# Three-layer CIN on one core: one gather row for both weights of a pair, W2 in one transfer, two field tiles ahead of the weight table

## The chip, the cores and the metric

The kernel runs on one core of a Trainium2 chip. The metric is the device time of one execution in microseconds (us), the median of nine runs. Engines are named as in the profile: PE is TensorE (PEld its weight loads), DVE is VectorE, ACT is ScalarE, POOL is GpSimd, SP is the sync engine. A name with q, as SPq, is an engine's instruction queue where it issues a DMA or waits.

## The reference

What is computed is a compressed interaction network of three layers on an embedding x of shape (1024, 39, 64), batch by fields by embedding:

```python
def _cin_layer(Xk, X0, W, b):
    O = W.shape[0]
    Hk, Fdim = (Xk.shape[1], X0.shape[1])
    Wr = W.reshape(O, Hk, Fdim)
    return jnp.einsum('bhe,bfe,ohf->boe', Xk, X0, Wr) + b[None, :, None]
X0 = sparse_embedding
Xk = X0
outs = []
for W, b in ((W0, b0), (W1, b1), (W2, b2)):
    Xk = _cin_layer(Xk, X0, W, b)
    outs.append(Xk.sum(axis=-1))
cin_output = jnp.concatenate(outs, axis=-1)
return cin_output @ fc_w.T + fc_b
```

W0 is (64, 39*39), W1 and W2 are (64, 64*39), fc_w is (1, 192), all in float32.

## The kernel before

**The mathematics.** The last two layers are linear in the layer before, and only their sum against fc_w is wanted. So the kernel folds W2 with fc_w into a matrix v2, and W1 with v2 into one weight per pair of fields. Each pair of fields (a, b) then has 128 weights: 64 of the first layer (from W0) and 64 of the folded rest. The main loop multiplies the products of field pairs with them. A pair (a, b) and a pair (b, a) have the same product, so their weights are added first.

**The main loop.** The batch is worked in 32 blocks of 32 samples, 2048 columns each. A block has six products of 128 pairs each (`PAIRS`, steps in the order 0, 1, 3, 2, 4, 5); a seventh product serves two blocks, 64 rows for each. `product` forms one on DVE from two tiles of gathered field rows: `rt[n % 2][:, i]`, i from 0 to 3, for the six, `ut` and `vt` for the seventh. `multiply` runs it through PE, four quarters of 512 columns, each of two passes. `finish` and `finish_quarter` multiply the two halves of the result and sum over the embedding. At the start the order is: three steps of block 0, three of block 1, then the rest of block 0, the seventh product, and the rest of block 1. Four product buffers exist (`prods`), and products are formed four steps ahead (`AHEAD`).

**How field rows arrive.** `load(n)` copies block n of x from HBM to a table `xd` in HBM, in pieces of 256 B, so that each field is a row of 8 KB. `roll(n, tiles)` then has POOL gather 128 such rows per tile by an indirect DMA (`lists` holds the row numbers), `roll_half(n)` does so for `ut` and `vt`.

**How weights arrive.** A second table in HBM, `table`, has a row of 128 floats for each ordered pair of fields (40 x 40 rows). It is written from the tiles `part` (two groups of 16 columns) and `rest` by three DMAs. `weights(c)` gathers from it twice for each of seven chunks, `wa` for (a, b) and `wb` for (b, a), by the row numbers in `wlists`; `add(c)` on DVE adds the two.

**The start.** All this is preceded by a chain of small steps, written out by hand on each queue. W2 is loaded in two halves of 64 partitions (`halves`), and so is W1. `fc2` holds a part of fc_w, copied there by ACT. Matmuls with `fc2` (line 278) fold W2; DVE transposes the result (line 289); `v2` takes it; matmuls with `v2` (lines 322 and 331) fold W1. `spin` runs matmuls without use, to keep PE at work. ACT copies W0 from `w0s` and `w0r` into `part` and `rest`, and DVE and ACT copy the folded part beside it. Then the table is written and gathered.

**What sets the order.** Each engine and each DMA-issuing queue works in program order (`manual_schedule`); waits between engines come from the tiles' accesses. DMAs of SP and ACT share eight semaphores in turn, and those of POOL another eight; a DMA waits until the earlier one of its semaphore has landed.

Of the kernel before, what the change touches and what calls it, by code (L numbers as in the profile page):

```python
# [58 lines left out]
FH = F * H  # L59
# [36 lines left out]
def cin_kernel(ctx: ExitStack, tc: tile.TileContext, x, w0t, b0, w1, b1, w2, b2, fc_w, fc_b, out):  # L96
# [16 lines left out]
    def load(n, engine=nc.sync):  # L113
        first = n % 2 * FT
        engine.dma_start(
            xd[n // 2 % NTAB][first : first + F].rearrange("f (b e) -> f b e", e=E),
            xv[:, n * BB : (n + 1) * BB, :],
        )
# [7 lines left out]
    def roll(n, tiles=range(4)):  # L126
        for i in tiles:
            gather_rows(rt[n % 2][:, i], n, n % 2 * 4 + i)
# [4 lines left out]

    wa = const.tile([128, NCHUNK, 2 * H], F32, name="wa")
    wb = const.tile([128, NCHUNK, 2 * H], F32, name="wb")
    fc = const.tile([H, 3], F32, name="fc")
# [7 lines left out]
    lists = const.tile([128, 10], I32, name="lists")  # L144
    wlists = const.tile([128, 2, NCHUNK], I32, name="wlists")
    rt = [const.tile([128, 4, BLK], F32, name=f"r{k}") for k in range(2)]
    ut = [const.tile([128, BLK], F32, name=f"u{k}") for k in range(2)]
    vt = [const.tile([128, BLK], F32, name=f"v{k}") for k in range(2)]

    table = dram.tile([FT * FT, 2 * H], F32, name="table")  # L150
    tablev = table.rearrange("(b a) h -> b a h", a=FT)

    prep = tc.tile_pool(name="prep", bufs=1)
    with prep as prep:
        w2s = prep.tile([128, FH // 2], F32, name="w2s")
        w1s = prep.tile([128, FH // 2], F32, name="w1s")
        fc2 = prep.tile([128, 32], F32, name="fc2")
        ones = prep.tile([16, 128], F32, name="ones")
# [7 lines left out]


        nc.gpsimd.iota(place, pattern=[[0, 1]], base=0, channel_multiplier=1)
        nc.vector.memset(warm, 0.0)
        nc.vector.memset(zeros, 0.0)  # L170
        nc.vector.memset(fc2, 0.0)  # L171
        nc.vector.memset(ones, 1.0)
        load(0, nc.gpsimd)
        nc.gpsimd.memset(w0s, 0.0)
        nc.gpsimd.memset(w0r, 0.0)
        load(1, nc.gpsimd)
        nc.gpsimd.memset(v2, 0.0)
        nc.gpsimd.memset(rest[:, NR], 0.0)

        def halves(dst, w):  # L180
            for s in range(2):
                nc.sync.dma_start(
                    dst[H * s : H * s + H], w[:, s * (FH // 2) : (s + 1) * (FH // 2)]
                )

        def load_ones(k, engine):
            for row in (F, FT + F):
                engine.dma_start(xd[k][row].rearrange("(p c) -> p c", c=128), ones)

        halves(w2s, w2)  # L190
        halves(w1s, w1)
        nc.scalar.dma_start(fc, fc_w.rearrange("o (l h) -> h (o l)", h=H))
        load_ones(0, nc.scalar)
        nc.scalar.copy(warm, warm)
        for k in range(2):
            nc.scalar.dma_start(w0s[H * k : H * k + F], w0t[:, NA * k : NA * (k + 1), :])
        nc.scalar.dma_start(w0r[0:F], w0t[:, 2 * NA : F, :])
        for s in range(2):
            nc.scalar.copy(fc2[H * s : H * s + H, 0:1], fc[:, 2:3])  # L199
            nc.scalar.copy(v2[H * s : H * s + H, F:FT], fc[:, 1:2])  # L200
# [8 lines left out]
        def spin(n):  # L209
            for _ in range(n):  # L210
                nc.tensor.matmul(idle, zeros[:, 0:128], zeros, start=True, stop=True)  # L211
# [14 lines left out]
        def step(x, at, by, out=None):  # L226

            out = new() if out is None else out
            nc.vector.tensor_scalar(out, x, at, by, ALU.is_ge, ALU.mult)
            return out  # L230

        def fused(out, x, scalar, y, op0, op1):
            nc.vector.scalar_tensor_tensor(out, x, scalar, y, op0, op1)
# [19 lines left out]
        nc.vector.tensor_scalar(lists[:, 4:8], fields_of[:, 0:4], float(FT), None, ALU.add)  # L253
        roll(0, (0, 1, 2))
        roll(1, (0, 1))

        step(row, HR, 1.0, half)
        fused(q, half, -float(HR), row, ALU.mult, ALU.add)
        nc.vector.tensor_tensor(field[4], q, step(q, F, -float(F)), ALU.add)
        nc.vector.tensor_tensor(field[4], field[4], step(q, 56, 11.0), ALU.add)  # L260
        nc.vector.tensor_scalar(field[5], q, float(F), None, ALU.min)
        fused(t, q, -50.0, step(q, 45, 1.0), ALU.add, ALU.mult)
        for y in (t, step(q, 50, -float(F)), step(q, 56, -6.0)):
            nc.vector.tensor_tensor(field[5], field[5], y, ALU.add)

        nc.vector.tensor_scalar(half, half, float(FT), None, ALU.mult)
        nc.vector.tensor_scalar(lists[:, 8:10], fields_of[:, 4:6], half, None, ALU.add)

# [5 lines left out]
        for k in range(2):  # L274
            for u in range(4):
                rows = slice(u % 2 * H, u % 2 * H + H)
                f0 = u // 2 * 19 + k * 10
                nc.tensor.matmul(  # L278
                    pv[k][32 * u : 32 * u + 32, 0:320],
                    fc2[rows],  # L280
                    w2v[rows, f0 : f0 + 10, :],
                    start=True,
                    stop=True,
                )
# [13 lines left out]

        nc.vector.tensor_scalar(scaled, fields_of, float(FT), None, ALU.mult)
        pair = prep.tile([128, 4], F32, name="pair")  # L300
        nc.vector.tensor_scalar(wlists[:, 0, 0:3], scaled[:, 1:4], field[0], None, ALU.add)
        nc.vector.tensor_scalar(wlists[:, 1, 0:3], fields_of[:, 1:4], scaled[:, 0:1], None, ALU.add)
        nc.vector.tensor_tensor(wlists[:, 0, 3:5], scaled[:, 2:4], fields_of[:, 1:3], ALU.add)
        nc.vector.tensor_tensor(wlists[:, 1, 3:5], scaled[:, 1:3], fields_of[:, 2:4], ALU.add)
        for m, (i, k) in enumerate(((1, 3), (3, 1), (4, 5), (5, 4))):
            nc.vector.tensor_tensor(pair[:, m : m + 1], scaled[:, k : k + 1], field[i], ALU.add)
        fused(wlists[:, 0, 5:6], extra, float(NONE), pair[:, 0:1], ALU.mult, ALU.max)
        fused(wlists[:, 1, 5:6], extra, float(NONE), pair[:, 1:2], ALU.mult, ALU.max)
        last = step(q, 62, float(NONE))
        nc.vector.tensor_tensor(wlists[:, 0, 6:7], pair[:, 2:3], last, ALU.max)  # L310
        nc.vector.tensor_scalar(t, q, float(F), float(NONE), ALU.is_lt, ALU.mult)
        nc.vector.tensor_tensor(pair[:, 3:4], pair[:, 3:4], t, ALU.max)
        nc.vector.tensor_tensor(wlists[:, 1, 6:7], pair[:, 3:4], last, ALU.max)

# [14 lines left out]
        for s in range(2):  # L329
# [3 lines left out]
            )  # L333
        spin(9)
        for s, copy in enumerate((nc.vector.tensor_copy, nc.scalar.copy)):
# [5 lines left out]
            )  # L341
        nc.sync.dma_start(tablev[:, 0:NA, :], part[0:FT])
        nc.scalar.dma_start(tablev[:, NA : 2 * NA, :], part[H : H + FT])
        nc.sync.dma_start(tablev[:, 2 * NA : FT, :], rest[0:FT])
        for k in range(1, NTAB):
# [3 lines left out]
    def weights(c):  # L349
        for k, w in enumerate((wa, wb)):  # L350
            nc.gpsimd.indirect_dma_start(  # L351
                w[:, c], None, table[:], bass.IndirectOffsetOnAxis(ap=wlists[:, k, c : c + 1], axis=0)
            )

    weights(0)
    weights(1)
    weights(3)
    roll(1, (2,))
    weights(2)
    roll(0, (3,))  # L360
    weights(4)
    weights(5)
    roll_half(0)
    weights(6)
    roll(1, (3,))
# [16 lines left out]
    def multiply(n, c, p, quarters=range(BLK // MM)):  # L382
        half = c == NPAIR
        for k in (n, n + 1) if half else (n,):
            if k not in po:
                po[k] = [bank("po") for _ in range(BLK // MM)]
        for m in quarters:

            for h in range(2 if half else 1):
                w = slice(h * HR, (h + 1) * HR) if half else slice(0, 128)  # L390
                nc.tensor.matmul(  # L391
                    po[n + h][m],
                    wa[w, c, :],
                    p[w, bass.ts(m, MM)],
                    start=c == opens[n + h],
                    stop=c == closes[n + h],
                )
# [47 lines left out]

    def add(c):
        nc.vector.tensor_tensor(wa[:, c], wa[:, c], wb[:, c], ALU.add)

    AHEAD = 4
# [14 lines left out]
    last_weights()  # L464
    p = {s: product(*s) for s in steps[:2]}
    added = set()

    def add(c):
        if c not in added:
            added.add(c)  # L470
            nc.vector.tensor_tensor(wa[:, c], wa[:, c], wb[:, c], ALU.add)  # L471

    add(steps[0][1])
    p[steps[2]] = product(*steps[2])
    add(steps[1][1])
    add(steps[2][1])
    p[steps[3]] = product(*steps[3])
    fields(0)
# [76 lines left out]
```

## Time and profile before

| | us |
|---|---|
| median of nine runs (lowest, highest) | 766.96 (765.55, 768.89) |
| the profiled execution, its own time | 765.15 |
| its span in the profile | 763.3 |
| PE busy | 745.1 |
| main loop's matmuls (line 391), busy | 724.1 |
| DVE busy | 641.4 |
| POOL busy | 321.4 |
| table's DMAs issued | 16.84 to 17.68 |
| first gather from the table issued | 28.09 |
| first main matmul | 33.98 |

Times in the profile are counted from the start of its span; the execution's own time is 1.85 us longer than the span. A group's line gives its busy time and the idle time of its engine just before it, with what ended that wait. A piece of the chain says when it began, how long it took and which instruction or transfer it was. PE's matmuls of 32-bit floats appear as two records each. The granted clock of PE is 1 or one half; the mean was 0.991.

### The profile page before, as it was taken

The numbers are of one execution on the slowest core, as the hardware profiler recorded it, in microseconds if no ns is written. First come the engines' busy times: TensorE is split into PE (matmuls) and PEld (weight loads), VectorE is DVE, ScalarE is ACT, GpSimd is POOL, SyncE is SP. The second block draws the span as 40 slices with busy tenths as digits, with TensorE's granted clock in tenths as the row PEclk, the third lists the DMA queues.
The fourth block names the chain that finished last, engine by engine and source line by source line (L and its number), as shares of the span: only waits on it lengthen the run. The fifth ranks groups of instructions, "written<-read, shape, count | busy, mean of one in ns | idle before, by whom it ended". The sixth has DMA issues, their size and how long they took to land.

```text
span 763.3 us, 5146 instructions
## 1 busy us (share of the span) xinstructions
PE 745.1 (98%) x1856; PEld 322.3 (42%) x1856; DVE 641.4 (84%) x479; ACT 160.4 (21%) x207; POOL 321.4 (42%) x185
## 2 busy tenths in 40 slices
PE   6599999999999999999999999999999999999998
PEld 2244444444444444444444444444444444444443
DVE  6376988898888888988888988888998888898885
ACT  2002312211221211222121222212122221212212
POOL 4488173633436354243625425363432536334200
PEclk9799999999999999999999999999999999999999
DMA  8849968565876657687575768657577764737400
GB/s 259 270 172 392 389 212 333 188 276 185 327 253 233 263 188 271 213 330 248 203 288 167 273 244 321 237 190 291 177 282 253 282 261 155 272 151 311 166 0 0
DMA packets 62839, 181.79 MB, mean 238 GB/s; under 512 B 41364, under 2 KB 41499, under 8 KB 42254
## 3 DMA queue, kind: packets, MB, share of 16 engines
q0 software_dynamic: 23712, 169.34, 57.9%
q1 hardware_dynamic: 38494, 11.36, 6.4%
q10 hardware_dynamic: 608, 0.77, 0.3%
q8 instruction: 14, 0.23, 0.1%
q14 instruction: 11, 0.09, 0.0%
HBM read 180.58 MB, written 11.10 MB: 251 GB/s over the span
## 4 chain that ended last, share of the span: by engine, by line
PE 92%; DMA 4%; issue 2%; POOL 1%; DVE 0%; ACT 0%; SPq 0%; POOLq 0%; DVEq 0%
PE po L391 91%; DMA table<-rest 1%; DMA u<-xd,lists 1%; POOL wb L351 1%; DMA fc<-in_fc_w 1%; POOL wa L351 1%; DMA b0s<-in_b 1%; DMA wa<-table,wlists 1%; DMA wb<-table,wlists 0%; PE pv L278 0%; PE pt L322 0%; POOL r L122 0%; DVE blocks L289 0%; PE pr L331 0%; DVE g L430 0%
## 5 line engine op out<-in xcount | busy, mean ns | idle before, releaser
L391 PE MATMUL po<-p,wa 128*128 128x512 f32 (+1 forms) x1792 | 724.1, 596 | 9.0 <-DVE wa L471 9.0
L377 DVE TENSOR_TENSOR p<-r 128x2048 f32<-128x2048 f32 x192 | 434.6, 2290 | 91.0 <-PE po L391 83.8
L391 PEld LDWEIGHTS po<-p,wa 128*128 128x128 f32 (+1 forms) x1792 | 314.9, 190 | 417.5 <-issue 395.8
L122 POOL DMA_INDIRECT r<-xd,lists x128 | 249.7, 1951 | 362.3 <-DVE p L377 335.9
L410 ACT ACTIVATE x<-po,b0s 64x512 f32<-64x512 f32 x124 | 84.5, 684 | 354.4 <-PE po L391 347.9
L404 ACT COPY g<-u 39x1024 f32<-39x1024 f32 x64 | 66.6, 1043 | 215.0 <-DVE sums L421 181.2
L416 DVE SCALAR_TENSOR_TENSOR g<-po,fc,x 64x512 f32<-64x512 f32 x124 | 86.4, 734 | 0.0
L421 DVE TENSOR_REDUCE sums<-g 103x16 f32<-103x1024 f32 x62 | 75.6, 1220 | 2.2
L379 DVE TENSOR_TENSOR p<-u,v 128x2048 f32<-128x2048 f32 x16 | 36.5, 2284 | 5.5 <-DMA v<-xd,lists 5.5
L122 POOL DMA_INDIRECT u<-xd,lists x16 | 30.7, 1919 | 4.9 <-issue 4.6
L122 POOL DMA_INDIRECT v<-xd,lists x16 | 16.0, 999 | 4.9 <-issue 4.9
L351 POOL DMA_INDIRECT wa<-table,wlists x7 | 10.5, 1503 | 14.2 <-DMA table<-rest 12.4
L211 PE MATMUL idle<-zeros 128*128 128x512 f32 x24 | 13.1, 692 | 1.5 <-DVE fc L171 1.5
L351 POOL DMA_INDIRECT wb<-table,wlists x7 | 10.3, 1478 | 2.1 <-issue 2.1
L471 DVE TENSOR_TENSOR wa<-wa,wb 128x128 f32<-128x128 f32 x7 | 2.0, 286 | 9.1 <-DMA wa<-table,wlists 7.0
L211 PEld LDWEIGHTS idle<-zeros 128*128 128x128 f32 x24 | 5.0, 220 | 8.2 <-issue 6.8
L430 DVE SCALAR_TENSOR_TENSOR g<-po,fc,x1q 64x512 f32<-64x512 f32 x4 | 3.0, 743 | 5.3 <-ACT x1q L429 5.3
L278 PE MATMUL pv<-w2s,fc 64*32 64x320 f32 x16 | 2.8, 764 | 4.4 <-DMA b0s<-in_b 4.4
L289 DVE STREAM_TRANSPOSE blocks<-pv 64x320 f32<-64x320 f32 x4 | 2.1, 514 | 3.7 <-issue 3.5
L429 ACT ACTIVATE x1q<-po,b0s 64x512 f32<-64x512 f32 x4 | 2.7, 684 | 10.2 <-PE po L391 10.2
L278 PEld LDWEIGHTS pv<-w2s,fc 64*32 64x32 f32 x16 | 1.0, 142 | 6.6 <-ACT fc L199 6.0
L432 DVE TENSOR_REDUCE sums<-g 103x8 f32<-103x512 f32 x4 | 2.7, 686 | 0.1
(74 smaller groups left out, 30.4 us busy)
## 6 DMA issues: line engine op xcount, KB each, us to landing
xd<-in_x SPq DMA_DIRECT2D x30, 312.0 KB
r<-xd,lists POOLq DMA_INDIRECT x128
w2s<-in_w SPq DMA_DIRECT2D x2, 312.0 KB
xd<-in_x POOLq DMA_DIRECT2D x2, 312.0 KB
w1s<-in_w SPq DMA_DIRECT2D x2, 312.0 KB
table<-part SPq DMA_DIRECT2D x1, 320.0 KB
table<-part ACTq DMA_DIRECT2D x1, 320.0 KB
w0s<-in_w0t ACTq DMA_DIRECT2D x2, 156.0 KB
```

Source lines behind the costliest of these rows:

```text
L122: nc.gpsimd.indirect_dma_start(dst, None, table, bass.IndirectOffsetOnAxis(ap=lists[:, k : k + 1], axis=0))
L211: nc.tensor.matmul(idle, zeros[:, 0:128], zeros, start=True, stop=True)
L278: nc.tensor.matmul(pv[k][32 * u : 32 * u + 32, 0:320], fc2[rows], w2v[rows, f0 : f0 + 10, :], start=True, stop=True,)
L351: nc.gpsimd.indirect_dma_start(w[:, c], None, table[:], bass.IndirectOffsetOnAxis(ap=wlists[:, k, c : c + 1], axis=0))
L377: nc.vector.tensor_tensor(p, rt[n % 2][:, i], rt[n % 2][:, k], ALU.mult)
L379: nc.vector.tensor_tensor(p, ut[n // 2 % 2], vt[n // 2 % 2], ALU.mult)
L391: nc.tensor.matmul(po[n + h][m], wa[w, c, :], p[w, bass.ts(m, MM)], start=c == opens[n + h], stop=c == closes[n + h],)
L404: nc.scalar.copy(gt[H : H + F], ut[n // 2 % 2][h : h + F, bass.ts(m, SUB)])
L410: nc.scalar.activation(x1[m // 2][:, bass.ts(m % 2, MM)], po[n][m][H:128], AF.Identity, bias=b0s[H:128])
L416: nc.vector.scalar_tensor_tensor(gt[0:H, at], po[n][m][0:H], fc[:, 0:1], x1[m // 2][:, at], ALU.add, ALU.mult)
L421: nc.vector.tensor_reduce(sums[:, b_at : b_at + SB], gt.rearrange("p (b e) -> p b e", e=E), AX.X, ALU.add)
L430: nc.vector.scalar_tensor_tensor(gt[0:H], po[n][m][0:H], fc[:, 0:1], t, ALU.add, ALU.mult)
```

## The change

The table's row is doubled to 256 floats: the first half of row (b, a) holds that pair's weights, the second half those of (a, b). Each half ("side") is written by its own three DMAs, six in all. One gather per chunk brings both halves into one tile `w`, and `add` adds the second half to the first; for the seventh chunk it adds under a mask, `apart`. The second list of row numbers goes away.

In the start, W2 comes in one transfer of 128 partitions in which output and half alternate; `fc2` is widened, spread to suit, and filled by two DMAs instead of ACT's copies; the line-278 matmuls take all 128 rows. load(0) moves from POOL to SP, behind W2. W1's halves and W0's parts are split over SP and ACT. Some memsets move from POOL to DVE. The list arithmetic for `lists[:, 8:10]` and `wlists` is done later. Ahead of the table POOL gathers two tiles (block 0, tiles 0 and 1) instead of five; block 0's tile 2 comes after weights(0), load(1) after weights(1), and block 1's tiles 0 to 2 after weights(3). weights(6) comes ahead of roll_half(0). `spin(9)` becomes `spin(13)`.

```diff
-    table = dram.tile([FT * FT, 2 * H], F32, name="table")
-    tablev = table.rearrange("(b a) h -> b a h", a=FT)
+    table = dram.tile([FT * FT, 4 * H], F32, name="table")
+    sides = (
+        table.rearrange("(b a) h -> b a h", a=FT)[:, :, 0 : 2 * H],
+        table.rearrange("(a b) h -> b a h", b=FT)[:, :, 2 * H : 4 * H],
+    )
...
-        load(0, nc.gpsimd)
         nc.gpsimd.memset(w0s, 0.0)
         nc.gpsimd.memset(w0r, 0.0)
-        load(1, nc.gpsimd)
-        nc.gpsimd.memset(v2, 0.0)
-        nc.gpsimd.memset(rest[:, NR], 0.0)
...
-        halves(w2s, w2)
-        halves(w1s, w1)
-        nc.scalar.dma_start(fc, fc_w.rearrange("o (l h) -> h (o l)", h=H))
+        fcv = fc_w.rearrange("o (l h) -> h (o l)", h=H)
+        for s, engine in enumerate((nc.sync, nc.scalar)):
+            engine.dma_start(fc2[s:128:2, 32 * s : 32 * s + 1], fcv[:, 2:3])
+        nc.sync.dma_start(w2s, w2.rearrange("o (s n) -> (o s) n", s=2))
+        nc.scalar.dma_start(fc, fcv)
+        load(0)
         load_ones(0, nc.scalar)
+        for s, engine in enumerate((nc.sync, nc.scalar)):
+            engine.dma_start(
+                w1s[H * s : H * s + H], w1[:, s * (FH // 2) : (s + 1) * (FH // 2)]
+            )
+        for k, engine in enumerate((nc.sync, nc.scalar)):
+            engine.dma_start(w0s[H * k : H * k + F], w0t[:, NA * k : NA * (k + 1), :])
+        nc.sync.dma_start(w0r[0:F], w0t[:, 2 * NA : F, :])
         nc.scalar.copy(warm, warm)
...
-            nc.scalar.copy(fc2[H * s : H * s + H, 0:1], fc[:, 2:3])
...
-        roll(0, (0, 1, 2))
-        roll(1, (0, 1))
...
+        roll(0, (0, 1))
...
-                    fc2[rows],
-                    w2v[rows, f0 : f0 + 10, :],
+                    fc2[:, u % 2 * 32 : u % 2 * 32 + 32],
+                    w2v[:, f0 : f0 + 10, :],
...
-        spin(9)
+        spin(13)
...
-        nc.sync.dma_start(tablev[:, 0:NA, :], part[0:FT])
-        nc.scalar.dma_start(tablev[:, NA : 2 * NA, :], part[H : H + FT])
-        nc.sync.dma_start(tablev[:, 2 * NA : FT, :], rest[0:FT])
+        for k, engine in enumerate((nc.sync, nc.scalar)):
+            for side in sides:
+                engine.dma_start(side[:, NA * k : NA * (k + 1), :], part[H * k : H * k + FT])
+        for side, engine in zip(sides, (nc.sync, nc.scalar)):
+            engine.dma_start(side[:, 2 * NA : FT, :], rest[0:FT])
...
     def weights(c):
-        for k, w in enumerate((wa, wb)):
-            nc.gpsimd.indirect_dma_start(
-                w[:, c], None, table[:], bass.IndirectOffsetOnAxis(ap=wlists[:, k, c : c + 1], axis=0)
-            )
+        nc.gpsimd.indirect_dma_start(
+            w[:, c], None, table[:], bass.IndirectOffsetOnAxis(ap=wlists[:, c : c + 1], axis=0)
+        )
 
     weights(0)
+    roll(0, (2,))
     weights(1)
+    load(1, nc.gpsimd)
     weights(3)
-    roll(1, (2,))
+    roll(1, (0, 1, 2))
     weights(2)
     roll(0, (3,))
     weights(4)
     weights(5)
+    weights(6)
     roll_half(0)
-    weights(6)
     roll(1, (3,))
     load(2)
     load(3)
...
-            nc.vector.tensor_tensor(wa[:, c], wa[:, c], wb[:, c], ALU.add)
+            one, other = w[:, c, 0 : 2 * H], w[:, c, 2 * H : 4 * H]
+            if c < NPAIR:
+                nc.vector.tensor_tensor(one, one, other, ALU.add)
+            else:
+                nc.vector.scalar_tensor_tensor(one, other, apart, one, ALU.mult, ALU.add)
```

More of the change, by code (lines that the diff above doesn't have):

```diff
@@ L132, in roll_half @@
         gather_rows(vt[n // 2 % 2], n, 9)
-    wa = const.tile([128, NCHUNK, 2 * H], F32, name="wa")
-    wb = const.tile([128, NCHUNK, 2 * H], F32, name="wb")
+    w = const.tile([128, NCHUNK, 4 * H], F32, name="w")
     fc = const.tile([H, 3], F32, name="fc")
@@ L144, in cin_kernel @@
     lists = const.tile([128, 10], I32, name="lists")
-    wlists = const.tile([128, 2, NCHUNK], I32, name="wlists")
+    wlists = const.tile([128, NCHUNK], I32, name="wlists")
+    apart = const.tile([128, 1], F32, name="apart")
     rt = [const.tile([128, 4, BLK], F32, name=f"r{k}") for k in range(2)]
@@ L156, in cin_kernel @@
         w1s = prep.tile([128, FH // 2], F32, name="w1s")
-        fc2 = prep.tile([128, 32], F32, name="fc2")
+        fc2 = prep.tile([128, H], F32, name="fc2")
         ones = prep.tile([16, 128], F32, name="ones")
@@ L168, in cin_kernel @@
         nc.gpsimd.iota(place, pattern=[[0, 1]], base=0, channel_multiplier=1)
[L169 to L172, printed above, removed]
-        load(0, nc.gpsimd)
         nc.gpsimd.memset(w0s, 0.0)
         nc.gpsimd.memset(w0r, 0.0)
-        load(1, nc.gpsimd)
-        nc.gpsimd.memset(v2, 0.0)
-        nc.gpsimd.memset(rest[:, NR], 0.0)
[L180 to L183, printed above, removed]
-                )
+        nc.vector.memset(fc2, 0.0)
+        nc.vector.memset(zeros, 0.0)
+        nc.vector.memset(warm, 0.0)
+        nc.vector.memset(ones, 1.0)
+        nc.vector.memset(v2, 0.0)
+        nc.vector.memset(rest[:, NR], 0.0)
         def load_ones(k, engine):
@@ L188, in load_ones @@
                 engine.dma_start(xd[k][row].rearrange("(p c) -> p c", c=128), ones)
-        halves(w2s, w2)
-        halves(w1s, w1)
-        nc.scalar.dma_start(fc, fc_w.rearrange("o (l h) -> h (o l)", h=H))
-        load_ones(0, nc.scalar)
+        fcv = fc_w.rearrange("o (l h) -> h (o l)", h=H)
[4 more added lines that the diff above has]
+        load(0)
+        load_ones(0, nc.scalar)
+        for s, engine in enumerate((nc.sync, nc.scalar)):
[5 more added lines that the diff above has]
+        nc.sync.dma_start(w0r[0:F], w0t[:, 2 * NA : F, :])
         nc.scalar.copy(warm, warm)
-        for k in range(2):
-            nc.scalar.dma_start(w0s[H * k : H * k + F], w0t[:, NA * k : NA * (k + 1), :])
-        nc.scalar.dma_start(w0r[0:F], w0t[:, 2 * NA : F, :])
         for s in range(2):
-            nc.scalar.copy(fc2[H * s : H * s + H, 0:1], fc[:, 2:3])
             nc.scalar.copy(v2[H * s : H * s + H, F:FT], fc[:, 1:2])
@@ L253, in cin_kernel @@
         nc.vector.tensor_scalar(lists[:, 4:8], fields_of[:, 0:4], float(FT), None, ALU.add)
-        roll(0, (0, 1, 2))
-        roll(1, (0, 1))
[L257 to L267, printed above, removed]
+        roll(0, (0, 1))
         blocks = prep.tile([H, F * 32], F32, name="blocks")
@@ L275, in cin_kernel @@
             for u in range(4):
-                rows = slice(u % 2 * H, u % 2 * H + H)
                 f0 = u // 2 * 19 + k * 10
@@ L296, in cin_kernel @@
         nc.scalar.copy(rest[:, 0:NR, H : 2 * H], w0r.rearrange("b (a h) -> b a h", h=H))
[L299 to L313, printed above, removed]
+        step(row, HR, 1.0, half)
+        fused(q, half, -float(HR), row, ALU.mult, ALU.add)
+        nc.vector.tensor_tensor(field[4], q, step(q, F, -float(F)), ALU.add)
+        nc.vector.tensor_tensor(field[4], field[4], step(q, 56, 11.0), ALU.add)
+        nc.vector.tensor_scalar(field[5], q, float(F), None, ALU.min)
+        fused(t, q, -50.0, step(q, 45, 1.0), ALU.add, ALU.mult)
+        for y in (t, step(q, 50, -float(F)), step(q, 56, -6.0)):
+            nc.vector.tensor_tensor(field[5], field[5], y, ALU.add)
+        nc.vector.tensor_scalar(half, half, float(FT), None, ALU.mult)
+        nc.vector.tensor_scalar(lists[:, 8:10], fields_of[:, 4:6], half, None, ALU.add)
         w1v = w1s.rearrange("o (h f) -> o f h", f=F)
@@ L341, in cin_kernel @@
             )
-        nc.sync.dma_start(tablev[:, 0:NA, :], part[0:FT])
-        nc.scalar.dma_start(tablev[:, NA : 2 * NA, :], part[H : H + FT])
-        nc.sync.dma_start(tablev[:, 2 * NA : FT, :], rest[0:FT])
+        for k, engine in enumerate((nc.sync, nc.scalar)):
[3 more added lines that the diff above has]
+            engine.dma_start(side[:, 2 * NA : FT, :], rest[0:FT])
+        nc.vector.tensor_scalar(scaled, fields_of, float(FT), None, ALU.mult)
+        pair = prep.tile([128, 2], F32, name="pair")
+        nc.vector.tensor_scalar(wlists[:, 0:3], scaled[:, 1:4], field[0], None, ALU.add)
+        nc.vector.tensor_tensor(wlists[:, 3:5], scaled[:, 2:4], fields_of[:, 1:3], ALU.add)
+        for m, (i, k) in enumerate(((1, 3), (4, 5))):
+            nc.vector.tensor_tensor(pair[:, m : m + 1], scaled[:, k : k + 1], field[i], ALU.add)
+        fused(wlists[:, 5:6], extra, float(NONE), pair[:, 0:1], ALU.mult, ALU.max)
+        fused(wlists[:, 6:7], step(q, 62, 1.0), float(NONE), pair[:, 1:2], ALU.mult, ALU.max)
+        step(q, F, 1.0, apart)
         for k in range(1, NTAB):
@@ L349, in weights @@
     def weights(c):
-        for k, w in enumerate((wa, wb)):
-            nc.gpsimd.indirect_dma_start(
-                w[:, c], None, table[:], bass.IndirectOffsetOnAxis(ap=wlists[:, k, c : c + 1], axis=0)
-            )
+        nc.gpsimd.indirect_dma_start(
+            w[:, c], None, table[:], bass.IndirectOffsetOnAxis(ap=wlists[:, c : c + 1], axis=0)
+        )
     weights(0)
+    roll(0, (2,))
     weights(1)
+    load(1, nc.gpsimd)
     weights(3)
-    roll(1, (2,))
+    roll(1, (0, 1, 2))
     weights(2)
@@ L389, in multiply @@
             for h in range(2 if half else 1):
-                w = slice(h * HR, (h + 1) * HR) if half else slice(0, 128)
+                rows = slice(h * HR, (h + 1) * HR) if half else slice(0, 128)
                 nc.tensor.matmul(
                     po[n + h][m],
-                    wa[w, c, :],
-                    p[w, bass.ts(m, MM)],
+                    w[rows, c, 0 : 2 * H],
+                    p[rows, bass.ts(m, MM)],
                     start=c == opens[n + h],
@@ L444, in last_weights @@
         nc.scalar.activation(kfin, pk[0:1, 0:1], AF.Identity, bias=fcb, scale=float(E))
-    def add(c):
-        nc.vector.tensor_tensor(wa[:, c], wa[:, c], wb[:, c], ALU.add)
     AHEAD = 4
@@ L464, in cin_kernel @@
     last_weights()
-    p = {s: product(*s) for s in steps[:2]}
+    p = {steps[0]: product(*steps[0])}
     added = set()
@@ L470, in add @@
             added.add(c)
-            nc.vector.tensor_tensor(wa[:, c], wa[:, c], wb[:, c], ALU.add)
+            one, other = w[:, c, 0 : 2 * H], w[:, c, 2 * H : 4 * H]
[3 more added lines that the diff above has]
+                nc.vector.scalar_tensor_tensor(one, other, apart, one, ALU.mult, ALU.add)
     add(steps[0][1])
[L474 to L477, printed above, removed]
+    for k in (1, 2, 3):
+        p[steps[k]] = product(*steps[k])
+        if k < 3:
+            add(steps[k][1])
     fields(0)
```

## The prediction

> **What bounds the kernel now.** I read the page's busy times first, then the chain of waits, then the timeline of the first 70 us, then what the DMA queues moved in single stretches.
>
> ```profile
> PE 745.1 (98%) x1856; PEld 322.3 (42%) x1856; DVE 641.4 (84%) x479; ACT 160.4 (21%) x207; POOL 321.4 (42%) x185
> L391 PE MATMUL po<-p,wa 128*128 128x512 f32 (+1 forms) x1792 | 724.1, 596 | 9.0 <-DVE wa L471 9.0
> ```
>
> TensorE works for 724.1 us in the main loop and waits 9.0 us ahead of it, 8.7 of them before its first matmul. From there to the end of the loop it has no other hole than 0.27 us. So the change, which touches only the start, moves the end by what it moves the moment from which TensorE never waits again. The timeline gives the stations on the way:
>
> ```profile
> 9.67 1.04 POOL L122 DMA_INDIRECT r<-xd,lists  x1 [4.46 <-DMA xd<-in_x]
> 9.68 2.83 PE L278 MATMUL pv<-w2s,fc 64*32 64x320 f32 x16 [4.41 <-DMA b0s<-in_b]
> ...
> 16.88 7.99 PE L211 MATMUL idle<-zeros 128*128 128x512 f32 x18
> ...
> 28.09 0.94 POOL L351 DMA_INDIRECT wa<-table,wlists  x1 [12.36 <-DMA table<-rest]
> ...
> 33.98 11.44 PE L391 MATMUL po<-p,wa 128*128 128x512 f32 x19 [8.78 <-DVE wa L471]
> ...
> 37.16 0.95 POOL L122 DMA_INDIRECT r<-xd,lists  x1 [0.30 <-DMA wa<-table,wlists]
> ...
> 47.60 2.29 DVE L377 TENSOR_TENSOR p<-r 128x2048 f32<-128x2048 f32 x1 [0.23 <-PE po L391]
> ...
> 64.65 0.28 DVE L471 TENSOR_TENSOR wa<-wa,wb 128x128 f32<-128x128 f32 x1
> 64.99 45.27 PE L391 MATMUL po<-p,wa 128*128 128x512 f32 x119 [0.27 <-DVE wa L471]
> ```
>
> Fields' weights start at 9.68, the table's last write is issued at 17.41, POOL gathers from it at 28.09, TensorE starts at 33.98. The product at 47.60 waits for a free buffer, which is the end of the third step (0,3): so step (1,0) starts at about 47.4. Adding the 0.27 hole, the old schedule counts as one in which (1,0) starts at **47.6** and nothing waits later. That is the number to beat.
>
> ```profile
> 17.41 9.96 DMA table<-rest
> 33.10 3.85 DMA wa<-table,wlists
> 52.27 6.88 DMA u<-xd,lists
> ```
>
> The longest piece of the chain is the table's landing. The five gathers ahead of it and the table share the DMA engines:
>
> ```profile
> DMA packets 367, 2.74 MB, mean 343 GB/s; under 512 B 32, under 2 KB 32, under 8 KB 32
> q0 software_dynamic: 366, 2.74, 100.5%
> ```
>
> This is 12 to 20 us: POOL's queue alone fills all 16 engines.
>
> [...] the landing records of the first write of part hold ten increments, 24.19 to 25.17 us. [...] packets of 8192 B take 309 ns, of 512 B 27 ns, of 256 B 18 ns. [...] w2s ran at 199 GB/s from 2 to 5 us, gathers into 128 partitions at 343[...]. [...] Here it was half from 29.9 to 40.1 us, after the spins ended at 24.9.
>
> **W2 and x.** Before, w2s landed by 6.88, but the matmuls at 9.68 waited for ACT's copies of fc, queued behind ACT's w0s issue at 8.06. Now fc2 is filled by two small DMAs (0.6 us of issue each, as a bias load), so w2s is issued at 1.6 instead of 0.74. With eight packets per engine from about 3.0 and the same 1 us from last packet to landing I put it at 6.2 (bounds 5.5 and 7.6), hence pv at 6.6: 3.1 us earlier. It also falls into full clock, -0.5 us on the way to pt (bounds 0 and -0.9). Matmuls of 128 rows instead of 64 are taken as equal in time, since the old row shows 16 of 763 ns in 2.83 us, four or so at once (bounds -0.9 and +1.4, half the row). load(0) goes from POOL to SP, behind w2s on one queue: data 6.0 to 7.8, landing 1 us later, so the first gather is issued at about 8.8 instead of 9.67 (bounds 7.8 and 10.3). w1s's second half, w0s, bias wait for an earlier DMA of the same semaphore, as bias did before (1.3 us behind fc); w1s should land near 10, just as v2 is ready at 6.6+3.7=10.3. ACT's copy of w0s into part (1.05) must come before its pt copy; w0s lands by 11, which leaves a microsecond. The list arithmetic that moved (14 small DVE instructions of 0.15, 2 us) lies under pt and pr (3 us); if that cover is gone it adds 2 us at most. memsets moved to DVE: 0.4 us, before the lists, which are ready at 6.1, still before load(0). The old last issue was 7.73 after pv began; now, with one more DMA on each queue (0.6), it is 6.6+7.73-0.5+0.6 = 14.4, the first at 13.2.
>
> **The table.** Bytes double to 1.64 MB, and rows of 1 KB with a half written by each side turn 8 KB packets into 512 B ones: 3200 on ten engines is 320 each, by 27 ns = **8.6 us** (before: 40+40 of 8192 B and 40 of 4096 B, 4 each: 4x309x2+4x159 = 3.1 us of work, but shared with gathers). Two gathers precede it instead of five. In the old trace two took from 11.44 to 18.0; 0.9 earlier they end at 17.1. The old table's first packet came 3.9 us after its issue, behind gathers; 13.2+3.9 = 17.1 too. So the table has the engines to itself from 17.1, ends 25.7, lands 0.9 later (as before): **T = 26.6** against 27.37. Bounds: gathers over at 15.5 and 25 ns each give 24.4; 29 ns and a start at 18 give 28.2; strided HBM writes have no row here, 36 ns would give 29.5.
>
> **After the table.** POOL spends 1.25 us per gather (0.95+0.30). Seven gathers fewer free 8.8 us of POOL time, but what matters is the order. From T: weights(0) at +0.7, r0 tile 2 to +2.9, weights(1), load(1) to +5.6. weights(0) is one gather: landing +4.3, add, first matmul at +4.9 (old +6.6). Its step needs r0 tile 2 next: landing +7.5 (the tile issued at 37.16 landed at 42.76, 4.65 after its issue ended), product +9.9; at half clock step (0,0) ends at +11.8 anyway. Three steps of 3.43 plus about 3 of cold clock end at +18.2. Block 1 is now late: roll(1) may only start when load(1) has landed. POOL's old loads landed 5.6 and 6.3 us after their issue ended: +11.2. Tiles 0 and 1 are issued to +12.5 and +13.7; the first lands 4.65 later, the second 3.25 after it (as v after u), +20.4; product 2.29: (1,0) starts at **T+22.7**. TensorE stands still for some 4.5 us there. What is queued behind POOL's wait, weights(2), r0 tile 3, u, v, is needed at +32.9 or later and lands by +26 to +33; u and v are needed at +43. [...]
>
> The sum: 26.6+22.7 = 49.3 against 47.6 is +1.7 us[...]. **+2.0 us**. On the profiled execution (765.15, span 763.3) that is 767.2; it was 1.8 under the median, so on 766.96 it is **769.0**.
>
> **Rivals.** Faster: the table is out early. If load(0) lands at 7.8 and the gathers end at 15.5, T is 24.4, and if load(1), with no W1 or W2 beside it, lands 4 us after issue, (1,0) starts at T+21.1 = 45.5: -2.1 us, 764.9. For it: the idle engines after T (36 to 39 us of the old trace moved a mean of 54 GB/s). Against it: 4992 packets of loads 2 to 5 come at that time. It decides where T plus the delay falls under 47.6 - 1.5 = 46.1. No difference: T=26, delay 21.6, +0.0, 767.0; early start and late block 1 cancel. Much slower: 512 B writes at 36 ns, T=29.5, (1,0) at 52.2: +4.6, 771.6. That the seven gathers themselves bring time is excluded by the waits: only weights(0) is on the path, where it saves 1.25.
>
> **Chances.** About 0.2% (1.5 us) is what a measurement of this kernel can tell from no change. Slower by more: 0.54 (the likeliest, 768.5 to 772; with small writes slow up to 774). Within: 0.26. Faster: 0.20. Range 764.8 to 773.0.
>
> **To check.** pv near 6.6; first gather near 8.8; last table landing near 26.6; no spin longer than to 25; first main matmul near 31.5; a hole of 4 to 5 us ahead of (1,0) with its product waiting for a landing of r, POOL waiting there for xd; no hole later. Wrong if the table lands before 25 or load(1) holds nobody up.

## The result and the profile after

The changed kernel takes **771.86 us** (median of ten executions, 771.05 to 774.45) against 766.97 for the kernel before (31 executions): ratio 1.0063, 95% interval 1.0050 to 1.0075, so 4.9 us slower. Its profiled execution took 772.29, with a span of 770.5.

The page's busy times and the main loop's group, as before:

```profile
PE 750.7 (97%) x1864; PEld 324.4 (42%) x1864; DVE 640.8 (83%) x474; ACT 159.9 (21%) x205; POOL 310.7 (40%) x175
L389 PE MATMUL po<-p,w 128*128 128x512 f32 (+1 forms) x1792 | 726.6, 598 | 12.3 <-DVE w L468 8.2
```

The main loop's idle time is 12.3 us instead of 9.0: 8.2 ahead of the first matmul, and a new 4.1. The timeline (start, duration, engine, what it does, in brackets the wait ahead of it and its releaser) shows the stations. A step (n, c) is product c of block n, and T is the landing of the last table write:

```profile
7.78 2.56 PE L266 MATMUL pv<-w2s,fc 128*32 128x320 f32 x16 [2.46 <-DMA w2s<-in_w]
...
10.83 1.10 POOL L122 DMA_INDIRECT r<-xd,lists  x1 [8.55 <-DMA bias<-in_b]
...
15.97 6.11 ACTq L330 DMA_DIRECT2D table<-rest  x1
...
30.06 0.94 POOL L347 DMA_INDIRECT w<-table,wlists  x1 [16.88 <-DMA xd<-ones]
...
34.59 13.47 PE L389 MATMUL po<-p,w 128*128 128x512 f32 x24 [8.15 <-DVE w L468]
...
40.42 0.95 POOL L122 DMA_INDIRECT r<-xd,lists  x1 [4.57 <-DMA xd<-in_x]
...
49.86 2.29 DVE L375 TENSOR_TENSOR p<-r 128x2048 f32<-128x2048 f32 x1 [6.70 <-DMA r<-xd,lists]
...
52.20 23.08 PE L389 MATMUL po<-p,w 128*128 128x512 f32 x47 [4.15 <-DVE p L375]
```

POOL's first gather from the table comes at 30.06. The releaser named there isn't the real one, since the gather doesn't read what those ones fill. By the landing records the last table write lands at 29.29, and POOL starts 0.77 later (before: 27.37, then 28.09); in e1_load1_early, e7_spin22 and e8_start_wide the same delay is 0.76 to 0.77. After weights(3) POOL stands still for 4.57 us, until load(1) has landed in xd; block 1's first product waits for its tile to 49.86, and TensorE stands still for 4.15 us. The chain of waits says the same in two pieces (start, duration, what):

```profile
33.50 6.66 DMA xd<-in_x
...
41.68 8.16 DMA r<-xd,lists
```

A last line, the stretch right after that hole (us, length, busy time of PE, PEld, DVE, ACT, POOL, then the granted clock):

```profile
52.20:58.00 5.80, 5.80 (x8) 2.46 (x9) 5.50 (x3) 0.00 (x0) 5.00 (x3) 0.54 0.61 230
```

The granted clock had dropped to half in the hole, at 50.73, and stayed there until 57.56. At 0.54 of full speed over these 5.80 us TensorE loses 2.7 us more. Between the two profiled executions the main loop's end moved by 7.0 us: 0.6 from the later first matmul, 3.9 from the holes and 2.5 from matmuls that ran longer, which is the clock.

### The profile page after: what moved, and what is told of

The parts are those of the page before. It is cut to its first block, busy times and chain, and to the rows that moved or that the text cites. A ratio compares the mean times of both kernels' runs of the same rounds, so it can differ in the third digit from the quotient of the medians.

```text
span 770.5 us, 5145 instructions
## 1 busy us (share of the span) xinstructions
PE 750.7 (97%) x1864; PEld 324.4 (42%) x1864; DVE 640.8 (83%) x474; ACT 159.9 (21%) x205; POOL 310.7 (40%) x175
## 4 chain that ended last, share of the span: by engine, by line
PE 93%; DMA 4%; ACTq 1%; DVE 1%; issue 0%; POOL 0%; ACT 0%; SPq 0%
PE po L389 93%; DMA r<-xd,lists 1%; DMA xd<-in_x 1%; DMA xd<-ones 1%; ACTq L330 1%; DMA w2s<-in_w 1%; PE pv L266 0%; DVE p L375 0%; PE pt L306 0%; POOL w L347 0%; ACTq L184 0%; DVE blocks L277 0%; POOL r L122 0%; DVE g L428 0%; DVE sums L430 0%
## 5 line engine op out<-in xcount | busy, mean ns | idle before, releaser
L389 PE MATMUL po<-p,w 128*128 128x512 f32 (+1 forms) x1792 | 726.6, 598 | 12.3 <-DVE w L468 8.2
L389 PEld LDWEIGHTS po<-p,w 128*128 128x128 f32 (+1 forms) x1792 | 315.8, 191 | 422.3 <-issue 396.8
L122 POOL DMA_INDIRECT r<-xd,lists x128 | 252.8, 1975 | 378.0 <-DVE p L375 341.5
L213 PE MATMUL idle<-zeros 128*128 128x512 f32 x32 | 16.3, 662 | 1.5 <-DVE zeros L176 1.5
L347 POOL DMA_INDIRECT w<-table,wlists x7 | 8.4, 1196 | 18.7 <-DMA xd<-ones 16.9
L468 DVE TENSOR_TENSOR w<-w 128x128 f32<-128x128 f32 x6 | 1.7, 284 | 11.6 <-DMA w<-table,wlists 11.6
L213 PEld LDWEIGHTS idle<-zeros 128*128 128x128 f32 x32 | 6.3, 206 | 10.2 <-issue 8.7
L266 PE MATMUL pv<-w2s,fc 128*32 128x320 f32 x16 | 2.6, 767 | 2.5 <-DMA w2s<-in_w 2.5
L427 ACT ACTIVATE x1q<-po,b0s 64x512 f32<-64x512 f32 x4 | 2.7, 684 | 10.2 <-PE po L389 10.2
```

What stands on the lines that cost most here:

```text
L122: nc.gpsimd.indirect_dma_start(dst, None, table, bass.IndirectOffsetOnAxis(ap=lists[:, k : k + 1], axis=0))
L266: nc.tensor.matmul(pv[k][32 * u : 32 * u + 32, 0:320], fc2[:, u % 2 * 32 : u % 2 * 32 + 32], w2v[:, f0 : f0 + 10, :], start=True, stop=True,)
L347: nc.gpsimd.indirect_dma_start(w[:, c], None, table[:], bass.IndirectOffsetOnAxis(ap=wlists[:, c : c + 1], axis=0))
L389: nc.tensor.matmul(po[n + h][m], w[rows, c, 0 : 2 * H], p[rows, bass.ts(m, MM)], start=c == opens[n + h], stop=c == closes[n + h],)
```

## The experiments

Ratios are to runs of the kernel before on the same chip, whose medians there were 767.9 to 768.5 us. They are not quotients of the medians given here, from which they differ by up to 0.0015. Theory A: block 1's tiles wait for load(1), which POOL issues after the table. Theory B: the late table alone is what costs.

**Where load(1) stands.** `e1_load1_early` moves it to the front of POOL's DMAs:

```diff
+        load(1, nc.gpsimd)
         roll(0, (0, 1))
...
     weights(1)
-    load(1, nc.gpsimd)
     weights(3)
```

> The changed kernel with one line moved: POOL issues load(1) ahead of its first two gathers instead of after weights(1). Theory A (block 1's tiles wait for load(1), and that sets when TensorE runs without a hole): POOL doesn't stop after weights(3); counted from the table's landing T, the tiles of block 1 are issued to T+6.7 and T+8, land near T+12 and T+15.3, and step (1,0) starts where the third step ends, near T+18.8 instead of T+22.9. T itself stays within 1 us of 29.3. Expected 766 to 768 us, 4 to 6 less than the changed kernel. Theory B (the late table alone is what costs): the hole isn't decisive, and the time stays within 1 us of 771.9.

Measured: 767.29 us, ratio 0.9994 (0.9979 to 1.0008). Its timeline:

```profile
33.20 0.95 POOL L348 DMA_INDIRECT w<-table,wlists  x1 [17.56 <-DMA xd<-ones]
...
38.21 0.94 POOL L122 DMA_INDIRECT r<-xd,lists  x1 [0.30 <-issue]
...
44.53 15.72 PE L389 MATMUL po<-p,w 128*128 128x512 f32 x36 [1.90 <-DVE w L468]
```

The table is 3.1 us *later* than in the changed kernel (load(0) now lands beside load(1), at 12.5 instead of 10.0, and the first gather comes at 13.4), so the expectation on T failed. Yet POOL goes on without a wait, the only hole left is 1.90 us ahead of step (0,1), and the kernel gains 0.7%, about 5 us, on the changed one. B falls.

`e5_load1_sp` puts load(1) on SP behind w0r instead, out of load(0)'s way:

```diff
         nc.sync.dma_start(w0r[0:F], w0t[:, 2 * NA : F, :])
+        load(1)
...
     weights(1)
-    load(1, nc.gpsimd)
     weights(3)
```

> The changed kernel with load(1) on SP behind w0r, so that it delays neither load(0) nor block 1's tiles. Theory A (wait for load(1) at POOL): the first gather stays near 10.8, the first gather from the table near 30, and nothing but tile 2 of block 0 holds TensorE up; 3 us less than the version with load(1) first on POOL, whose table gather came at 33.2: 763.5 to 766 us. Theory B (that version gained because the table's writes met other traffic): 767 us or more.

Measured: 765.94 us, ratio **0.9974** (0.9962 to 0.9986): faster than the kernel before.

```profile
31.05 0.95 POOL L348 DMA_INDIRECT w<-table,wlists  x1 [17.44 <-DMA xd<-in_x]
...
36.06 0.94 POOL L122 DMA_INDIRECT r<-xd,lists  x1 [0.30 <-issue]
...
43.07 17.43 PE L389 MATMUL po<-p,w 128*128 128x512 f32 x40 [1.84 <-DVE w L468]
```

POOL goes on to block 1's tiles without a wait, and one hole of 1.84 us is left, for tile 2 of block 0, as A expected. The first gather (11.26) and the table gather are 0.4 and 1.0 us later than in the changed kernel. In this trace SP's second table write was issued only at 23.97, after a wait of 8.4 us for a table write of ACT to land: with one more DMA on SP the two had come to share a semaphore. The trace of the changed kernel has such a wait too: its w0r carries the semaphore of w2s and was issued at 7.71, after a wait of 1.7 us that ended when w2s landed at 7.65.

**The table alone.** `e2_wide_before` is the kernel before with the doubled table, its six writes and its seven gathers, and nothing else:

```diff
-    table = dram.tile([FT * FT, 2 * H], F32, name="table")
+    table = dram.tile([FT * FT, 4 * H], F32, name="table")
...
-        nc.sync.dma_start(tablev[:, 0:NA, :], part[0:FT])
+        for k, engine in enumerate((nc.sync, nc.scalar)):
+            for side in sides:
+                engine.dma_start(side[:, NA * k : NA * (k + 1), :], part[H * k : H * k + FT])
...
```

> The kernel before with nothing but the doubled table row, its six writes and seven gathers; start, five tiles ahead of the table and all orders as before. If 512 B packets are what makes the table late, they are starved by gather packets of 8 KB until those end near 30 us, the last landing comes near 37 instead of 27.4, and the kernel needs 774 to 777 us. If instead half the gathers from the table were a gain on the path and the writes were hidden, 764 to 766 us. If it is only the extra 5.5 us of packets on ten engines, some 770 us.

Measured: 771.02 us, ratio 1.0039 (1.0025 to 1.0054).

```profile
37.30 0.95 POOL L349 DMA_INDIRECT w<-table,wlists  x1 [21.23 <-DMA xd<-in_x]
...
41.92 18.65 PE L389 MATMUL po<-p,w 128*128 128x512 f32 x39 [16.26 <-DVE w L468]
```

The mechanism is the first that was expected, small packets starved by five gathers (42 to 71 of them started per us beside these, over 400 afterwards), and the table gather comes 9.2 us later, at 37.3. But it costs only some 3 us where 7 to 10 were expected with it, so the time alone would have fitted the third expectation: after 41.92 this kernel's TensorE has no hole at all. Against the second trace of the kernel before (e12_before_again, further down) its main loop starts 8.3 us later and ends 2.6 us later. That trace lost 3.7 us in a hole which this kernel doesn't have, and its main loop's matmuls took 1.9 us more in all (724.3 against 722.4), with a lower mean granted clock (0.984 against 0.993).

**The order without the table.** `e3_narrow` is the changed kernel with the old table, its three writes and its fourteen gathers:

```diff
...
-        nc.gpsimd.indirect_dma_start(
-            w[:, c], None, table[:], bass.IndirectOffsetOnAxis(ap=wlists[:, c : c + 1], axis=0)
-        )
+        for k, w in enumerate((wa, wb)):
+            nc.gpsimd.indirect_dma_start(
+                w[:, c], None, table[:], bass.IndirectOffsetOnAxis(ap=wlists[:, k, c : c + 1], axis=0)
+            )
...
```

> The changed kernel with the table as before (one half per row, three writes of 8 KB and 4 KB packets, two gathers per chunk); start, two tiles ahead and the order of tiles and loads as changed. Theory A: T falls from 29.3 to 23.5-24.5, but seven more POOL gathers of 1.25 us stand in the way (three of them before load(1) and block 1's tiles), so (1,0) starts at T+25.5, near 49.5 instead of 52.2: 768 to 770 us. Theory B (the table alone costs): the whole 5 us of T come back, 766 to 767 us.

Measured: 773.32 us, ratio 1.0076 (1.0051 to 1.0101): no better than the changed kernel, so both expectations failed.

```profile
24.32 0.95 POOL L350 DMA_INDIRECT wa<-table,wlists  x1 [12.32 <-DMA table<-rest]
...
48.07 18.95 PE L392 MATMUL po<-p,wa 128*128 128x512 f32 x40 [4.20 <-DVE p L378]
...
58.52 2.10 POOL L122 DMA_INDIRECT u<-xd,lists  x1 [0.30 <-issue]
...
68.90 2.29 DVE L380 TENSOR_TENSOR p<-u,v 128x2048 f32<-128x2048 f32 x1 [8.91 <-DMA v<-xd,lists]
...
71.45 4.11 PE L392 MATMUL po<-p,wa 128*128 128x512 f32 x5 [4.43 <-DVE wa L469]
```

The table is 5.7 us earlier, and all of it is lost again: the same wait for block 1 (4.20 us), and a second hole of 4.43, because POOL reaches u and v only at 58.5 (53.3 in the changed kernel). Seven gathers fewer *are* worth time in this order, in which those of weights(6) also stand ahead of u and v.

`e6_narrow_load1_sp` is that kernel with load(1) on SP and weights(6) after u and v.

> As the run before, and the table as in the kernel before (three large writes, fourteen gathers), with weights(6) after u and v as there. If POOL's queue, at 1.25 us and more per gather, is what made the narrow table slow in the changed order (u and v issued at 58.5 and 60.9, a hole of 4.4 us at 67), that hole goes with the wait for load(1): table gather near 24.5, first main matmul near 30, 762 to 766 us. If POOL's fourteen gathers stay in the way, a hole of several us stays near 67 and it needs 768 to 771 us.

Measured: 768.95 us, ratio 0.9995 (0.9974 to 1.0017), single executions from 764.3 to 770.1. Table gather 25.48, first main matmul 31.82, and holes of 0.36, 0.89 and, ahead of 66.57, 2.69 us. So the two moves together are worth 0.8% here (they weren't tried apart), and the fourteen gathers still leave u and v late. The time and the last hole fit the second expectation.

**The start alone.** `e4_start_only` gives the kernel before the new start:

```diff
-        halves(w2s, w2)
+        for s, engine in enumerate((nc.sync, nc.scalar)):
+            engine.dma_start(fc2[s:128:2, 32 * s : 32 * s + 1], fcv[:, 2:3])
+        nc.sync.dma_start(w2s, w2.rearrange("o (s n) -> (o s) n", s=2))
...
-        load(0, nc.gpsimd)
+        load(0)
...
```

> The kernel before with the new start alone: W2 in one transfer, fc2 by two DMAs, matmuls of 128 rows, load(0) on SP, W1 and W0 split over SP and ACT, memsets on DVE; table, five tiles ahead and orders as before. Theory A: pv starts near 7.8 instead of 9.7, but gathers start 1.2 us later (10.8), and both the table's landing and the last tiles follow the gathers: 766.5 to 768.5 us. Rival (the start is the gain of the change and the table eats it): 764 to 765.5 us.

Measured: 768.50 us, ratio 1.0003 (0.9989 to 1.0016): nothing. pv starts at 6.65 (before 9.68), but the first gather at 13.45 (before 9.67), 2.6 us later than expected; as in e1_load1_early, load(1) runs beside load(0) here.

`e8_start_wide` has start and doubled table in the old order.

> New start and doubled table in the old order: five tiles and load(1) ahead of the table. It fills the table of combinations. Theory A: the table lands behind the gathers near 38, as with the doubled table alone (first table gather 37.3), and TensorE then runs without a hole: 770 to 772.5 us. If start and table help each other as the changed kernel assumes, 768 us or less.

Measured: 773.61 us, ratio 1.0071 (1.0046 to 1.0097); table gather at 40.08, first main matmul 44.28, no hole after it. The median is 1.1 us over the expected range, and the table was 2 us later than I took it.

**The clock.** `e7_spin22` is the changed kernel with `spin(22)`.

> The changed kernel with spin(22) instead of spin(13): TensorE spins until about 33.7 and its clock should be full at the first main matmul. Theory A: nothing is gained, since step (0,1) waits for a product ready at 40.55 and block 1 for load(1): 771 to 773 us. Rival (the cold clock from 34.6 to 40.5 is part of the loss): 3 us less, 768.5 to 769.5 us.

Measured: 771.35 us, ratio 1.0039 (1.0025 to 1.0053). The clock stays full from 11 us on; the two waits remain:

```profile
39.78 7.13 PE L389 MATMUL po<-p,w 128*128 128x512 f32 x16 [2.03 <-DVE w L468]
...
50.57 1.98 PE L389 MATMUL po<-p,w 128*128 128x512 f32 x4 [3.66 <-issue]
```

The first half-clock stretch (30.25 to 40.49 us in the trace of the changed kernel) becomes a wait of 2.03 us for step (0,1), as A said. The second (50.73 to 57.56) is gone. The ratio is 0.0024 (1.8 us) under that of the changed kernel, with intervals that just overlap; the size fits the 2.7 us of the profiled execution, but is not firmly told apart from nothing. The trace is no typical one either: its execution (768.15) is the fastest of 20.

The length of a hole doesn't tell alone whether the clock falls. Here it stayed full through 3.66 us; in e6_narrow_load1_sp a hole of only 2.69 us, to 66.57, was followed by half clock from 67.57 to 70.98.

**Toward a better version.** All three of these have load(1) on SP. `e9_load0_pool` also puts load(0) back on POOL as its first DMA; `e10_load0_pool_spin22` adds spin(22) to e9; `e11_three_ahead` is e9 with three tiles ahead of the table.

> The version with load(1) on SP, and load(0) back on POOL as in the kernel before, as its first DMA (all else as changed). Theory (load(0) behind W2 on SP makes the first gather 1.2 us late, and the table waits for the gathers): first gather at 9.7 instead of 11.3, first table gather near 29.5 instead of 31.1, 1.5 us less than the version it is made from: 763.5 to 765 us. Rival (POOL's load takes W2's engines, pv comes later and the table with it): no gain, 766 us or more.

Measured: 765.73 us, ratio **0.9971** (0.9959 to 0.9983).

```profile
9.44 1.01 POOL L122 DMA_INDIRECT r<-xd,lists  x1 [5.46 <-DMA xd<-in_x]
...
27.80 0.95 POOL L348 DMA_INDIRECT w<-table,wlists  x1 [16.11 <-DMA xd<-ones]
```

The trace moves as the theory says: first gather 1.8 us and table gather 3.3 us earlier than in e5_load1_sp. The median hardly does (0.9974 to 0.9971), between the two expectations. The two profiled executions differ by 3.3 us (767.35 and 764.08), just as their tables do, but the medians by 0.2: the first lies 1.4 us above its kernel's median, the second 1.6 below. So the traces don't tell how far apart the tables are in typical executions.

> The run before with spin(22): the clock should be full from the first main matmul on. If the first cold stretch is hidden behind the wait for tile 2 of block 0, the median stays within 0.7 us of the run before; if it is not, 2 to 3 us less.

Measured: 767.78 us, ratio 1.0002 (0.9989 to 1.0015), 0.3% worse than without, so neither expectation held. The trace doesn't show why. The spins hold TensorE until 34.4, although the first weights are being added at 31.89; but step (0,1), which waits for tile 2 anyway, starts at 39.39, as against 39.76 in the trace of e9. And the execution traced, 763.72, is the fastest of 22. The cause stays open.

> As the first run of this call, and tile 2 of block 0 also ahead of the table (three tiles). If every gather ahead of the table delays it by its own 3 us, the first table gather comes near 32.5, the wait for tile 2 (1.8 us) goes, and the sum is 0.5 to 1.5 us more than with two. If the table's writes get their turn beside a gather, 1.5 us less.

Measured: 767.06 us, ratio 0.9986 (0.9974 to 0.9998), 1.3 us more than with two tiles, as expected, though the intervals of the two overlap; table gather at 30.35, no hole. In line with a gather ahead of the table delaying it by about its own time (expected 3 us; 2.6 us between these two traces).

**The kernel before, again.** `e12_before_again` is a second trace of it.

> The kernel before, unchanged, for a second trace: its executions spread from 764 to 772 us, and its first profiled one (765.15) lay 1.8 us under its median, so differences between single traces and between medians don't agree. If the spread comes from the waits near 65 us (u and v late, then the sum of weights behind them), this trace shows holes there of 1 to 5 us instead of 0.27; if it comes from the clock, a longer half-clock stretch with no such holes.

Its ten executions had a median of 766.95 (764.70 to 771.40), ratio to the others 0.9984 (0.9962 to 1.0007). This is a kernel against itself, so 0.16% in a comparison of this size is nothing. The profiled one took 768.56:

```profile
56.14 0.94 POOL L122 DMA_INDIRECT v<-xd,lists  x1 [0.30 <-issue]
...
64.16 2.29 DVE L379 TENSOR_TENSOR p<-u,v 128x2048 f32<-128x2048 f32 x1 [8.94 <-DMA v<-xd,lists]
...
66.71 13.52 PE L391 MATMUL po<-p,wa 128*128 128x512 f32 x34 [3.72 <-DVE wa L471]
```

v is issued 1.7 us later than in the first trace, lands 1.7 later, and the hole at its end is 3.72 us instead of 0.27. The two profiled executions differ by 3.4 us, which is this hole. So the kernel before does wait for u and v, by an amount that differs between executions; the first trace was one with almost none.

## Why the prediction was right or wrong

**Right in direction and order.** Slower, by block 1 waiting for load(1). From the table's last landing on, the steps came as worked out: first matmul T+5.3 (forecast +4.9), load(1) landed T+10.9 (+11.2), tile 1 of block 1 T+20.5 (+20.4), step (1,0) T+22.9 (+22.7), a hole of 4.15 us (4.5). e1_load1_early and e5_load1_sp show it by taking the wait away: 0.7 and 0.9% back.

**Luck in the median.** Two errors met, and in part cancelled. With T at 29.3 and the clock at 2.7 the same sum gives +7.3 us, close to the 7.1 between the profiled executions. But the forecast then added the 1.8 us by which the trace before lay under its median, and 774.3 would have been outside its range. The trace of the changed kernel lies 0.4 us above its median. That the difference of the medians is smaller by 2.2 us was not foreseen.

**Too small, 2.0 against 4.9 us.** In the profiled executions the step (1,0) came at 52.2 where 49.3 was forecast and 47.6 was the old one. The terms that were mis-sized:

- *w2s at 6.2, pv at 6.6*: w2s landed at 7.65, pv began at 7.78. The lateness is in the start: the first packets began 1.8 us after the issue ended, not 0.8, behind the small packets of fc2 on the same queue, which landed by 3.92. The 128 packets then started within 2.83 us (4.27 to 7.10), in two halves within 3.5 or more (from 2.10 to 5.61 at least, as the trace doesn't tell W2's packets from those of W1 behind them). Whether one transfer of 128 partitions is faster for its shape was not shown, since the traffic beside them differs.
- *The first gather at about 8.8*: 10.83. load(0) landed at 9.96, 1.2 us late, and POOL began 0.87 us after that. The trace before has such a delay (landed 8.85, gather at 9.67), and I left it out. This is most of T's error: the last gather packet ends at 19.9 instead of 17.1.
- *The table's 8.6 us*: packets are no slower than taken, a median of 27 ns for one of 512 B in both traces. 3200 at some 420 per us is 24 ns per engine, with ten engines taken from the ten increments in each table write's landing. But the two writes of rest needed 5.08 and 6.11 us to issue behind four full writes, and the last landing came 10.2 us after the first packet. T was 29.3 instead of 26.6. The rival with T = 29.5 gave 771.6, nearly the measured time, but its mechanism, slow small writes, is not what happened.
- *A second cold clock after that from 29.9 to 40.1 us, put at +0.3 as my estimate*: it came, for 2.7 us in the profiled execution, and perhaps 1.8 in typical ones by e7_spin22.

**Wrong on POOL's gathers.** "That the seven gathers themselves bring time is excluded by the waits" fell with e3_narrow: with fourteen gathers in the changed order a hole of 4.4 us appears at u and v. I had judged by a trace with a wait of 0.27 us there, without asking how far that zero was from the edge. The second trace of the kernel before has 3.72. That would also explain why the profiled executions differ by 7.1 us and the medians by 4.9: no trace with the doubled table has this wait, and the kernel before pays it in some executions. How often it pays was not measured.

**What the parts are worth**, as ratios to the kernel before:

| | old start | new start |
|---|---|---|
| old table, old order | 1 | 1.0003 |
| doubled table, old order | 1.0039 | 1.0071 |
| old table, two tiles ahead, load(1) late | not tried | 1.0076 |
| doubled table, two tiles ahead, load(1) late | not tried | 1.0063 |
| old table, two tiles ahead, load(1) on SP ahead of it, weights(6) after u and v | not tried | 0.9995 |
| doubled table, two tiles ahead, load(1) on SP ahead of it | not tried | 0.9974 |

The doubled table needs fewer tiles ahead of it: with five it loses 0.7%, with two it gains 0.26% once load(1) is not left behind the table. Whether the doubled table itself brings that gain is not settled, since the interval without it (0.9974 to 1.0017) overlaps the one with it (0.9962 to 0.9986). Why e9_load0_pool, with a table 3.3 us earlier in its trace, has no clearly better median stays open too.

## What to carry to other kernels

When a table is written ahead of time and work is put behind it, walk the issuing queue past it and ask of each entry what it must have landed: here one copy of 312 KB, put after the table, held up three gathers behind it and with them the main loop. A wait of nearly nothing in a trace is not a free wait: look at how close the two sides run, and take a second trace before calling a resource off the path. A trace is one execution: here single ones lay up to 4.1 us from their kernel's median, more than most of the differences in question. Spinning longer to keep the clock up did not clearly pay here: of the two tries one gained perhaps 0.24% and one lost 0.3%.

## What the runs showed of the hardware

In the changed kernel issuing a write of many small pieces was itself a wait: the first table write on each queue, 640 packets of 512 B, took 0.3 us to issue, and one of 320 such packets behind two of these took 5.1 us on SP and 6.1 on ACT (11.6 and 11.7 in e8_start_wide). Beside gathers of 8 KB packets such writes hardly moved: in e2_wide_before 42 to 71 of them started per us while the gathers ran (21 to 26 us), and over 400 once these had ended (27 to 29 us). Where POOL waited for several landings, it began an indirect gather 0.72 to 0.87 us after the last of them, in both kernels; after load(1), the only landing that it waited for at 40.16, it took 0.26 us.
